# A graph attention stack on one core: neighbour lists split by the upper and lower 64 rows, and more row tiles worked on over all nodes

## The chip, the core and the metric

The kernel runs on one core of a Trainium2 chip. TensorE (PE, with its weight loads as PEld), VectorE (DVE), ScalarE (ACT), GpSimd (POOL) and SyncE (SP) each work through their own queue and wait for one another by semaphores; SP and POOL issue nearly all DMAs. The metric is the device time of one execution in microseconds.

## The reference

Four graph attention layers follow one another on 4096 nodes with 256 features. `adj` (4096 x 4096) is one on the diagonal and, by chance, in one place of 256. Layers 0 and 1 have four heads of width 64, layer 2 two heads of width 128, layer 3 one score with a positive and a negative softmax. Cut to one layer:

```
h = x @ W                                   # per head
e = leaky_relu(s1[:, None] + s2[None, :])   # slope 0.2; s1, s2: dots of h with two vectors
att = softmax(where(adj, e, -inf), axis=1)
x = layernorm(x + att @ h)                  # layer 3: x + elu([att @ x, -att_neg @ x] @ fc_W)
```

## The kernel before

**Tiles and lists.** The nodes make 32 row tiles of 128 rows (P = 128, NT = 32). For a row tile, only nodes that at least one of its rows has as a neighbour matter, some 39% of all. `lists` (L293-486) reads the adjacency as int32, turns it into uint8 masks (L385), marks for each source tile j and row tile which nodes are hit (L389, `places` L394-425), counts their places with small matmuls, and packs (`pack`, L427-462). Packing builds a one-hot per source tile (L440) and multiplies it with the mask and three digits of the node number (L446), up to three list tiles per PSUM bank; ScalarE copies them out (L453). The result is, for each row tile, 13 list tiles of 128 nodes (NG = 13) with their masks (`maskC`) and node numbers (`idx`). `windows` (L106-127) bounds which list tiles a source tile can land in: the first six list tiles (FRONT) hold only nodes of the first 17 tiles (MIX). A count that does not fit raises a flag, upon which dense layers would run.

**A row tile of a layer** takes 14 positions, its own 128 nodes at position 6 and the 13 list tiles, in two halves of 7. `RowTile.load` (L632) has SP fetch the edge row S, the mask and the own rows, and POOL one indirect DMA per list tile (L647), each of which gathers 128 rows of `vals` (values and scores) into a slot `G`. `place` (L615) spreads the positions over slots from two pools (g0: 16, g1: 14), two positions per slot in layers 0 to 2 and one in layer 3. `half` (L651) makes the weights: ScalarE one activation per position and head, 128x128 (L712; L690 in layer 3), VectorE the products of the head that is kept as an exponential (L704, L708) and the mask (L681, with the mask copied to PSUM at L666; L714; L692, L694). TensorE then multiplies. In layers 0 and 1 the values are the stationary operand (65 columns) and the weights move (128), so the sum comes out transposed (L724), and `copy` and `back` (L744-758) turn it with ScalarE and four transposes. In layers 2 and 3 the 128x128 weights are stationary and 129 or 257 value columns move (L727). Every fp32 matmul is two records in the trace.

**Whole blocks.** Some blocks of four row tiles are worked on over all 32 source tiles instead of lists (`WHOLE`, L99: three blocks in layer 2, one in layer 3). `whole_rows` (L982) is a generator; one unit is one source tile, with 128x512 weights (L1016-1024) and matmuls for four row tiles (L1027). It needs no gathers.

**Order of the work.** Each engine's queue follows the program. `run` (L489) projects all 32 tiles for layer 0 while the first 10 lists are built (LEAD), then runs layer 0 and builds one further list per tile; `part` (L812) loads tiles m and m + 1 and then does half a tile, with the projection for the next layer of tiles that are done. `half_with_whole` (L859) adds units by a pace (`whole`, L804). `close` (L919) ends a layer and begins the next: it loads first halves of the next layer's tiles, finishes the last tile, and in layer 2 runs 10 units of layer 3 ahead. `norm` (L1049) normalises tiles in groups (GROUPS) with VectorE.

Of the kernel before, what the change touches and what calls it, by code (L numbers as in the profile page):

```python
# [70 lines left out]
NG = 13  # L71
NP = NG + 1
CAP = NG * P
HALF = NP // 2

GROUPS = (((24, 4),), ((28, 2),), ((16, 2), (17, 1), (20, 2), (24, 1), (31, 2)), ((28, 1), (31, 4)))
LEAD = 10
MIX = 17
FRONT = 6
NODES = tuple(MIX * P if t < FRONT else N for t in range(NG))  # L80
MC = P + 4
# [6 lines left out]

LOGS = (3, 3, 2, 1)
# [3 lines left out]
KEXP = 10.0  # L93

# [4 lines left out]
WHOLE = ((), (), (3, 7, 6), (7,))  # L99
# [6 lines left out]
def windows():  # L106

    share = 1.0 - (1.0 - 1.0 / 256.0) ** P
    mean, sd = P * share, (P * share * (1.0 - share)) ** 0.5
    dev = 4.5  # L110
    out = {}
    for m in range(NT):
        for j in range(NT):
            if j == m:
                continue
            if j < MIX:
                n = sum(q != m for q in range(j))
                lo = mean * n - dev * sd * n ** 0.5
                hi = mean * (n + 1) + dev * sd * (n + 1) ** 0.5
            else:  # L120
                n = sum(q != m for q in range(j, NT))
                lo = CAP - mean * n - dev * sd * n ** 0.5
                hi = CAP - mean * (n - 1) + dev * sd * (n - 1) ** 0.5
            a = max(0, int(lo // P))
            b = min(NG - 1, int((hi - 1) // P))
            out[m, j] = (a, b - a + 1)
    return out
# [3 lines left out]
assert all(a >= FRONT for (m, j), (a, _) in WINDOW.items() if j >= MIX)  # L131
WMAX = max(n for _, n in WINDOW.values()) * P
# [7 lines left out]
def kernel(ctx: ExitStack, tc: tile.TileContext, ins: dict, out: bass.AP):  # L140
# [11 lines left out]
        "shift2": const.tile([P, 1], F32, name="shift2"),  # L152
        "shift3": const.tile([4, 4], F32, name="shift3"),
        "zero": const.tile([4, 4], F32, name="zero"),
        "maskC": dram.tile([NT, P, NP, MC], U8, name="maskC"),
# [8 lines left out]
    nc.vector.memset(shared["shift2"], -2.0 * KEXP)  # L164

# [28 lines left out]
class Program:  # L194


    def __init__(self, tc, ctx, ins, out, shared):
        self.tc, self.nc, self.ins, self.out, self.shared = tc, tc.nc, ins, out, shared
        self.ctx = ctx
        self.wpool = self.pool("w", 2)  # L200
        self.small = self.pool("small", 1)
        self.io = self.pool("pio", 2)
        self.g0 = self.pool("g0", 16)
        self.wp = self.pool("wp", 5)
        self.ld = self.pool("ld", 4)
        self.ep = self.pool("ep", 2)
        self.ptwo = [self.pool(f"ptwo{k}", 2, space=PSUM) for k in range(2)]
        two, one, last = (self.pool(f"pair{k}", 2 - (k > 0), space=PSUM) for k in range(3))
        self.pfour, self.pthree, self.pmask = Turns((two, one, two, last)), Turns((two, one, two)), last
        self.masks = None  # L210
        self.banks = self.pfour
# [81 lines left out]
    def lists(self, ctx):  # L293
# [21 lines left out]
        for k, sh in enumerate((8, 4, 0)):  # L315
# [21 lines left out]
        nc.gpsimd.affine_select(out=bt[:, :, :MIX], in_=bt[:, :, :MIX], pattern=[[NT, BT], [1, MIX]],  # L337
                                compare_op=ALU.is_gt, fill=0.0, base=0, channel_multiplier=-1)
        nc.vector.tensor_scalar(bt[:, :, MIX:], bt[:, :, MIX:], -1.0, None, op0=ALU.mult)

        nc.gpsimd.affine_select(out=bt[:, :, MIX:], in_=bt[:, :, MIX:], pattern=[[-NT, BT], [-1, NT - MIX]],
                                compare_op=ALU.is_ge, fill=0.0, base=-MIX, channel_multiplier=1)


        lo = cst.tile([P, NT, NT], F16, name="lo")
        wid = cst.tile([P, NT, NT], F16, name="wid")
        nc.gpsimd.memset(lo, 0.0)
        nc.gpsimd.memset(wid, 0.0)
        for j in range(NT):
            m = 0  # L350
            while m < NT:
                if m == j:
                    m += 1
                    continue
                e = m
                while e < NT and e != j and WINDOW[e, j] == WINDOW[m, j]:
                    e += 1
                a, n = WINDOW[m, j]
                nc.gpsimd.memset(lo[:, m:e, j], a * P - 1.0 - (CAP if j >= MIX else 0))
                nc.gpsimd.memset(wid[:, m:e, j], float(n * P))  # L360
                m = e
        limit = cst.tile([P, NP], F32, name="limit")
        nc.vector.memset(limit[:, :FRONT], float(MIX * P - 1))
        nc.vector.memset(limit[:, FRONT:], float(N - 1))
        total = cst.tile([P, NT], F32, name="total")
        bad = cst.tile([P, BT, NT], F32, name="bad")
        nc.vector.memset(bad, 0.0)

        class Block:
            def __init__(self, blk):  # L370
                self.blk = blk
                self.mk = mkp.tile([P, NT, BT, MC], U8, name="mk")
                self.red = wk.tile([P, BT, NT], F32, name="red")

            def prepare(self, part):
# [5 lines left out]
                for q in range(q0, q1, 2):  # L381
# [4 lines left out]
                nc.vector.tensor_copy(mkw[:, q0:q1, :, P // 4:],  # L386
                                      digw[:, q0:q1].rearrange("p (j t o) -> p j t o", t=1, o=1)
                                      .to_broadcast([P, JG, BT, 1]))
                nc.vector.tensor_reduce(self.red[:, :, q0:q1].rearrange("p t j -> p j t"),  # L389
                                        mkw[:, q0:q1, :, :P // 4], AX.X, ALU.max)  # L390
# [3 lines left out]
            def places(self):  # L394
                blk = self.blk
                if any(blk in w for w in WHOLE):
                    nc.sync.dma_start(out=shared["maskW"][blk], in_=self.mk)
                hit = wk.tile([P, BT, NT], BF16, name="hit")
                nc.vector.tensor_scalar(hit, self.red, 0.0, None, op0=ALU.is_gt)
                flat = hit.rearrange("p t j -> p (t j)")  # L400
                nc.vector.memset(flat[:, blk * BT:blk * BT + (BT - 1) * (NT + 1) + 1:NT + 1], 0.0)
                pt = prog.bank(prog.pthree)
                nc.tensor.matmul(pt[:, :P], flat, ones, start=True, stop=True)
                totals = wk.tile([P, P], BF16, name="totals")
                nc.scalar.copy(totals, pt[:, :P])
                pq = prog.bank(prog.pthree)
                nc.tensor.matmul(pq[:, :P], tri, flat, start=True, stop=False, skip_group_check=True)
                nc.tensor.matmul(pq[:, :P], totals, bt.rearrange("p t j -> p (t j)"), start=False, stop=False,
                                 skip_group_check=True)
                nc.tensor.matmul(pq[:, P:P + BT], totals, tot, start=False, stop=True, skip_group_check=True)  # L410
                ms = slice(blk * BT, (blk + 1) * BT)
                self.place = wk.tile([P, BT, NT], F32, name="place")
                here = self.place
                nc.vector.tensor_tensor(here, pq[:, :P].rearrange("p (t j) -> p t j", t=BT), lo[:, ms, :],
                                        op=ALU.subtract)
                nc.vector.tensor_tensor(here, here, hit, op=ALU.mult)
                nc.vector.tensor_copy(total[:, ms], pq[:, P:P + BT])

                for col in (wid[:, ms, :], None):
                    off = wk.tile([P, BT, NT], F32, name="off")  # L420
                    if col is None:
                        nc.vector.tensor_scalar(off, here, 0.0, None, op0=ALU.is_lt)
                    else:
                        nc.vector.tensor_tensor(off, here, col, op=ALU.is_gt)
                    nc.vector.tensor_tensor(bad, bad, off, op=ALU.max)

            def pack(self, it):  # L427
                m, mk = self.blk * BT + it, self.mk
                cm = cmp_.tile([P, NP, MC], U8, name="cm")
                order = [j for j in range(NT) if j != m]  # L430
                touches = {}
                for j in order:
                    a, n = WINDOW[m, j]
                    for k in range(a, a + n):
                        touches.setdefault(k // 3, []).append((j, k))
                accs = {}
                for j in order:
                    a, n = WINDOW[m, j]
                    oh = ohp.tile([P, WMAX], BF16, name="oh")
                    nc.vector.tensor_scalar(oh[:, :n * P], iota[:, :n * P], self.place[:, it, j:j + 1], None,  # L440
                                            op0=ALU.is_equal)
                    for k in range(a, a + n):
# [3 lines left out]
                        nc.tensor.matmul(accs[b][:, s * MC:(s + 1) * MC], oh[:, (k - a) * P:(k - a + 1) * P],  # L446
                                         mk[:, j, it, :].bitcast(FP8), start=touches[b][0] == (j, k),
                                         stop=touches[b][-1] == (j, k), skip_group_check=True)
                        if touches[b][-1] == (j, k):
                            e = min(3, NG - 3 * b)  # L450
                            got = accs[b][:, :e * MC].rearrange("p (s c) -> p s c", c=MC)
                            o = 3 * b + (3 * b >= FRONT)
                            last = nc.scalar.activation(cm[:, o:o + e, :], got, AF.Copy, scale=EDGE / 2.0)  # L453

                with tc.issue_after(last.ins):
                    nc.scalar.copy(cm[:, FRONT, :], mk[:, m, it, :])
                nc.sync.dma_start(out=shared["maskC"][m], in_=cm)

                t = wk.tile([P, NP], F32, name="t")
                nc.vector.scalar_tensor_tensor(t, cm[:, :, P], 16.0, cm[:, :, P + 1], op0=ALU.mult, op1=ALU.add)  # L460
                nc.vector.scalar_tensor_tensor(t, t, 16.0, cm[:, :, P + 2], op0=ALU.mult, op1=ALU.add)
                nc.vector.tensor_tensor(shared["idx"][:, m, :], t, limit, op=ALU.min)
# [1127 lines left out]
```

## Time and profile before

| | us |
|---|---|
| runs shown | 2251.94, 2260.22, 2251.93; median 2251.94 |
| profiled execution, span | 2249.3 |
| busy in it: PE, PEld, DVE, ACT, POOL | 2014.0, 1834.3, 1786.6, 1737.9, 1494.4 |
| gathers (L647, 1456) | from 101.3 to 2219.6; mean 1.017 each |
| gathers of layers 0, 1, 2, 3 (416, 416, 260, 364) | from 101.3, 783.6, 1313.0, 1681.2 |

The profile is one execution, seen by instruction: line, engine, operation, output and inputs, start and length. A group's mean is the length of one instruction; since instructions of an engine overlap at their ends, the distance between starts is what one costs a full queue, and it is a little shorter. The profiled execution's own time is not measured apart from its span; the span is 2.6 us under the median of the runs, which hold what lies before the first and after the last instruction. "issue" means that the engine waited for nothing that the profile shows.

### The profile page before, as it was taken

Reading aid. Unit: us, or ns where it says so; the run is one execution under the profiler, and the core shown is the slowest. Engines: PE = TensorE matmul, PEld = TensorE weight load, DVE = VectorE, ACT = ScalarE, POOL = GpSimd, SP = SyncE. Lnnn points to the kernel's source line nnn. Section 1 sums busy time; section 2 is a strip of 40 time slices with the busy share of each in tenths; the row PEclk is TensorE's granted clock in tenths of the full one; section 3 lists DMA queues with packets and bytes.
Section 4 is the critical chain, followed back from the end, with each engine's and each line's share of the span. In section 5 each row is a group of like instructions: output and inputs, shape, how many; then the busy total and the mean of one; then the engine's idle time right before and its main releaser. Section 6 shows DMA issues by size and latency. Waiting matters only on the chain. (4 is left out here: it accounts for less than half of the span.)

```text
span 2249.3 us, 49137 instructions
## 1 busy us (share of the span) xinstructions
PE 2014.0 (90%) x15689; PEld 1834.3 (82%) x15689; DVE 1786.6 (79%) x5060; ACT 1737.9 (77%) x4989; POOL 1494.4 (66%) x1597
## 2 busy tenths in 40 slices
PE   4878889989999969988899898989999999999995
PEld 2658788878899859988888798989998888788784
DVE  2889899999999959987988886887876566566566
ACT  4778988988789859987888776987876677667664
POOL 2107655656677777777777777777773477777773
PEclk7999999999999989999999999999999999999998
DMA  8879877777566665666665666777777688888884
GB/s 284 258 245 360 272 219 250 254 247 228 146 170 191 174 202 168 182 175 175 173 185 162 172 167 171 226 209 223 223 227 225 200 282 280 249 284 270 262 248 130
DMA packets 250319, 492.99 MB, mean 219 GB/s; under 512 B 44385, under 2 KB 156610, under 8 KB 249666
## 3 DMA queue, kind: packets, MB, share of 16 engines
q0 software_dynamic: 81536, 245.30, 38.3%
q1 hardware_dynamic: 163906, 240.26, 33.3%
q10 hardware_dynamic: 4608, 4.20, 0.5%
q8 instruction: 126, 2.06, 0.4%
q14 instruction: 143, 1.17, 0.2%
HBM read 437.05 MB, written 52.54 MB: 218 GB/s over the span
## 5 line engine op out<-in xcount | busy, mean ns | idle before, releaser
L647 POOL DMA_INDIRECT G<-vals,idx x1456 | 1480.7, 1017 | 715.7 <-issue 221.1
L712 ACT ACTIVATE w<-S,G 128x128 f32<-128x128 f32 x3248 | 1001.6, 390 | 140.6 <-DMA G<-vals,idx 101.6
L724 PE MATMUL bank<-w,G 128*65 128x128 f32 x7168 | 837.8, 276 | 59.7 <-DVE w L681 59.3
L724 PEld LDWEIGHTS bank<-w,G 128*65 128x65 f32 x7168 | 798.7, 140 | 69.9 <-DVE w L681 68.4
L681 DVE SCALAR_TENSOR_TENSOR w<-w,bank 128x1792 f32<-128x1792 f32 x256 | 514.6, 2013 | 13.4 <-ACT w L712 11.2
L727 PE MATMUL bank<-G,w 128*128 128x257 f32 (+1 forms) x2660 | 490.8, 342 | 25.7 <-ACT z L1102 13.6
L727 PEld LDWEIGHTS bank<-G,w 128*128 128x128 f32 x2660 | 431.9, 195 | 73.2 <-ACT z L1102 16.4
L1027 PE MATMUL bank<-vw,pw 128*128 128x129 f32 (+1 forms) x2048 | 298.5, 301 | 3.7 <-issue 2.3
L1027 PEld LDWEIGHTS bank<-vw,pw 128*128 128x128 f32 x2048 | 273.6, 191 | 20.1 <-issue 2.8
L690 ACT ACTIVATE w<-S,G 128x128 f32<-128x128 f32 x385 | 137.8, 393 | 136.8 <-DMA G<-vals,idx 90.0
L440 DVE TENSOR_SCALAR oh<-iota,place 128x256 bf16<-128x256 f16 (+2 forms) x992 | 221.8, 298 | 9.4 <-PE bank L446 9.1
L704 DVE TENSOR_TENSOR w<-S,G 128x256 f32<-128x256 f32 x384 | 151.9, 416 | 69.9 <-DMA G<-vals,idx 66.5
L446 PE MATMUL bank<-mk,oh 128*128 128x132 fp8e4 x2336 | 192.1, 226 | 13.8 <-ACT cm L453 7.0
L557 PE MATMUL bank<-wext,xT 128*128 128x268 f32 (+3 forms) x640 | 176.9, 409 | 16.9 <-ACT xT L548 14.1
L446 PEld LDWEIGHTS <-oh 128*128 128x128 bf16 x2336 | 146.9, 99 | 50.4 <-DVE oh L440 12.7
L385 ACT ACTIVATE mk<-raw 128x1024 uint8<-128x1024 int32 x128 | 130.5, 1051 | 28.0 <-DMA raw<-in_adjB_dram 27.7
L557 PEld LDWEIGHTS bank<-wext,xT 128*128 128x128 f32 x640 | 117.2, 200 | 36.0 <-ACT xT L548 16.9
L1017 DVE SCALAR_TENSOR_TENSOR pw<-pw,mw 128x512 f32<-128x512 f32 x192 | 127.6, 689 | 18.2 <-ACT pw L1016 17.5
L1016 ACT ACTIVATE pw<-Sw,d 128x512 f32<-128x512 f32 x192 | 133.2, 711 | 7.5 <-PE bank L1027 7.0
L714 DVE SCALAR_TENSOR_TENSOR w<-w,mk 128x896 f32<-128x896 f32 x80 | 86.6, 1086 | 41.1 <-ACT w L712 37.9
L1024 DVE TENSOR_TENSOR pw<-pw,mw 128x512 f32<-128x512 f32 x64 | 43.6, 691 | 85.4 <-ACT pw L1023 48.0
L692 DVE TENSOR_TENSOR w<-w,mk 128x896 f32<-128x896 f32 x55 | 60.0, 1091 | 59.5 <-ACT w L691 58.2
(140 smaller groups left out, 1563.3 us busy)
## 6 DMA issues: line engine op xcount, KB each, us to landing
raw<-in_adjB_dram SPq DMA_DIRECT2D x128, 512.0 KB
mk<-maskC SPq DMA_DIRECT2D x112, 231.0 KB
G<-vals,idx POOLq DMA_INDIRECT x1456
S<-edge SPq DMA_DIRECT2D x64, 256.0 KB
vw<-vals SPq DMA_DIRECT2D x96, 129.0 KB
xp<-y SPq DMA_DIRECT2D x96, 128.0 KB
y<-xp SPq DMA_DIRECT2D x96, 128.0 KB
mw<-maskW SPq DMA_DIRECT2D x20, 528.0 KB
```

Source lines behind the costliest of these rows:

```text
L440: nc.vector.tensor_scalar(oh[:, :n * P], iota[:, :n * P], self.place[:, it, j:j + 1], None, op0=ALU.is_equal)
L446: nc.tensor.matmul(accs[b][:, s * MC:(s + 1) * MC], oh[:, (k - a) * P:(k - a + 1) * P], mk[:, j, it, :].bitcast(FP8), start=touches[b][0] ...
L557: nc.tensor.matmul(pp[:, :c1 - c0], self.xT[:, k, :], wext[:, k, c0:c1], start=(k == 0), stop=(k == KT - 1 and brow is None))
L647: nc.gpsimd.indirect_dma_start(out=self.place(pos), out_offset=None, in_=sh["v"][n][:NODES[t], :], in_offset=bass.IndirectOffsetOnAxis(ap= ...
L681: nc.vector.scalar_tensor_tensor(pair, pair, LEAST, mh2, op0=ALU.max, op1=ALU.mult)
L690: nc.scalar.activation(w[0][:, k, :], S[:, 0, :], AF.Relu, bias=d(k, 0))
L704: nc.vector.tensor_tensor(w[h][:, k:k + 2, :], S[:, h:h + 1, :].to_broadcast([P, 2, P]), dd[:, :, V + T + h:V + T + h + 1].to_broadcast([P ...
L712: nc.scalar.activation(w[h][:, k, :], S[:, h, :], AF.Exp, bias=d(k, h))
L724: nc.tensor.matmul(accs[0][:Wd, h * P:(h + 1) * P], v, w[h][:, k, :], **how)
L727: nc.tensor.matmul(a, w[h][:, k, :], v, **how)
L1016: nc.scalar.activation(p, S[:, h], AF.Exp, bias=d)
L1027: nc.tensor.matmul(accs[it][:, c:c + Wd], p[:, it, :], v[:, c:c + Wd], start=(j == 0 and h == heads[0]), stop=(j == NT - 1), skip_group_ch ...
```

## The change

The rows of a tile are taken as an upper and a lower 64. A node is in one of three classes: hit by upper rows only, by lower rows only, or by both. Lists become five pairs and three mixed tiles. In a pair, one gathered tile of 128 nodes serves the upper 64 rows and another the lower 64, and both share one 128x128 tile of weights and mask (a unit); mixed tiles and the own tile serve all rows. So a row tile has 14 gathered or own tiles as before but 9 units instead of 14: 4 in the first half (own, three pairs), 5 in the second (two pairs, three mixed). Nodes over the five pairs spill into the mixed tiles.

Activations and matmuls of a pair come as two of 64 rows (columns) each. In layers 0 and 1 the weights are now the stationary operand and 65 value columns move, so the sum comes out straight and `copy` and `back` are gone. Masks and weights are as long as the units: 512 and 640 columns per head instead of 896. Lists read from 23 instead of 17 tiles in their first half. Slots hold a whole half tile (layer 3: four positions), 4 + 4 slots instead of 16 + 14. Block 7 (row tiles 28-31) of layer 1 is worked on whole by a new generator `whole_heads`, which takes the weight as a maximum of two products instead of an exponential; in layer 3 block 6 (24-27) joins block 7. With a whole block in layer 1, its end runs as layer 2's does: ten units of layer 2 ahead.

```
-NG = 13
-NP = NG + 1
-CAP = NG * P
-HALF = NP // 2
+HP = P // 2
+NPAIR = 5
+NMIX = 3
+NPACK = NPAIR + NMIX
...
+HALF = 7
+FIRST = 3
+UNITS = (1 + FIRST, NPACK - FIRST)
+FULL = ((0,), tuple(range(NPAIR - FIRST, NPACK - FIRST)))
+PAIRS = (tuple(range(1, 1 + FIRST)), tuple(range(NPAIR - FIRST)))
...
-MIX = 17
-FRONT = 6
-NODES = tuple(MIX * P if t < FRONT else N for t in range(NG))
-MC = P + 4
+MIX = 23
+MC = P + 8
...
+TWOS = ((3, 0), (2, 1))
...
+PER = tuple(HALF if n < 3 else 4 for n in range(4))
+SLOT = max(p * r for p, r in zip(PER, ROW))
...
-WHOLE = ((), (), (3, 7, 6), (7,))
+WHOLE = ((), (7,), (3, 7, 6), (7, 6))
...
+    hit = 1.0 - (1.0 - 1.0 / 256.0) ** HP
+    one, both = hit * (1.0 - hit), hit * hit
...
+        n = max(j - 1, 0), min(j + 1, NT - 1)
+        lo, hi = reach(one, *n)
...
+        c, d = reach(both, *n)
+        if hi > cap:
+            c, d = min(c, least + max(0.0, lo - cap)), max(d, most + spill + hi - cap)
...
+        out.append((a, b - a + 1, e, f - e + 1))
...
-        self.g0 = self.pool("g0", 16)
+        self.g0 = self.pool("g0", 4)
...
-                nc.vector.tensor_copy(mkw[:, q0:q1, :, P // 4:],
...
-                nc.vector.tensor_reduce(self.red[:, :, q0:q1].rearrange("p t j -> p j t"),
-                                        mkw[:, q0:q1, :, :P // 4], AX.X, ALU.max)
+                for u in range(2):
+                    nc.vector.tensor_reduce(self.red[:, u, :, q0:q1].rearrange("p t j -> p j t"),
+                                            mkw[:, q0:q1, :, u * HP // 4:(u + 1) * HP // 4], AX.X, ALU.max)
...
+                here = wk.tile([P, 2, BT, NT], F32, name="here")
+                nc.vector.tensor_tensor(here, at[:, :2], each(lo, 2, BT, NT), op=ALU.subtract)
+                nc.vector.tensor_tensor(here, here, cls[:, :2], op=ALU.mult)
+                nc.vector.tensor_tensor(here, here, move, op=ALU.add)
...
+                    nc.vector.tensor_scalar(oh[:, :len(ks) * P], iota[:, :len(ks) * P], self.place[:, it, j:j + 1],
+                                            None, op0=ALU.is_equal)
...
-        self.g1 = self.pool("g1", 14)
+        self.g1 = self.pool("g1", 4)
...
+    def slot(self, half, s):
...
+            pool = L.prog.g1 if n > 0 and half else L.prog.g0
+            self.slots[half, s] = pool.tile([P, SLOT], F32, name="G")
...
+        for k in range(1 - half, HALF):
+            pos = half * HALF + k - 1
             nc.gpsimd.indirect_dma_start(
-                out=self.place(pos), out_offset=None, in_=sh["v"][n][:NODES[t], :],
+                out=self.place(half, k), out_offset=None, in_=sh["v"][n][:N if half else MIX * P, :],
                 in_offset=bass.IndirectOffsetOnAxis(ap=sh["idx"][:, m, pos:pos + 1], axis=0))
...
+    def parts(self, half):
+
+        out, k = {}, 0
+        for u in range(UNITS[half]):
+            if u in PAIRS[half]:
+                out[u] = [(slice(0, HP), self.place(half, k)), (slice(HP, P), self.place(half, k + 1))]
+                k += 2
+            else:
+                out[u] = [(slice(0, P), self.place(half, k))]
+                k += 1
+        return out
...
+            for u in range(U):
+                for rows, g in parts[u]:
+                    nc.scalar.activation(w[0][:, u, rows], S[:, 0, rows], AF.Relu, bias=d(g, 0))
...
+            turns = ((3, 0), (1, 2)) if n < 2 else ((0,), (1,))
+
+
+        for t, heads in enumerate(turns):
+            for us in (FULL[half], PAIRS[half])[::-1 if t == 1 and (half == 1 or n < 3) else 1]:
+                for h in heads:
+                    for u in us:
+                        for rows, g in parts[u]:
+                            a = accs[h][rows, :Wd] if n == 3 else accs[0][rows, h * Wd:(h + 1) * Wd]
+                            nc.tensor.matmul(a, w[h][:, u, rows], g[:, h * Wd:(h + 1) * Wd],
+                                             start=half == 0 and u == 0 and (n == 3 or h == turns[0][0]),
+                                             stop=half == 1, skip_group_check=True)
...
-            for m in range(4 if following.n == 3 else 1):
+            for m in range(4 if following.n == 3 else 2 if WHOLE[self.n] else 1):
...
+    def whole_heads(self):
...
+            for up, flat in TWOS:
+                bu, bf = prog.bank(prog.pwhole), prog.bank(prog.pwhole)
...
+                for j in range(NT):
+                    fetch(j + 4)
+                    mj = mws[j - j % JG][:, j % JG, :, :P]
+                    v = vs.pop(j)
+                    p = {}
+                    for h in (up, flat):
+                        p[h] = prog.dp.tile([P, BT, P], F32, name="pw")
+                        nc.vector.scalar_tensor_tensor(p[h], S[:, h], c[:, j, h:h + 1], mj, op0=ALU.max, op1=ALU.mult)
+                    how = dict(stop=j == NT - 1, skip_group_check=True)
+                    for it in range(BT):
+                        nc.tensor.matmul(bu[:, it * Wd:(it + 1) * Wd], p[up][:, it, :],
+                                         v[:, up * Wd:(up + 1) * Wd], start=j == 0 and it == 0, **how)
+                        nc.tensor.matmul(bf[:Wd, it * P:(it + 1) * P], v[:, flat * Wd:(flat + 1) * Wd],
+                                         p[flat][:, it, :], start=j == 0 and it == 0, **how)
+                    yield
...
```

## The prediction

> **What bounds the kernel now.** I read the page's busy shares first (TensorE 90%, VectorE 79%, ScalarE 77%, POOL 66%: nothing decides), then the starts of the gathers on POOL, which cut the run into stages, then the table by stretches for these stages. Its columns: stretch, length, busy us (and instructions) of PE, PEld, DVE, ACT and POOL, granted clock, DMA share, GB/s.
>
> ```profile
> 0.00:163.00 163.00, 113.77 (x975) 85.75 (x975) 108.73 (x484) 105.95 (x252) 19.43 (x146) 0.87 0.81 262
> 163.00:645.00 482.00, 430.68 (x4300) 394.31 (x4299) 464.96 (x1383) 417.00 (x1240) 307.28 (x302) 0.98 0.75 243
> 645.00:783.50 138.50, 130.71 (x1141) 125.49 (x1139) 127.33 (x305) 125.23 (x436) 104.73 (x108) 1.00 0.65 179
> 783.50:1313.00 529.50, 466.52 (x3916) 436.63 (x3917) 444.46 (x1003) 435.81 (x1465) 402.46 (x417) 0.96 0.63 177
> 1313.00:1681.00 368.00, 348.66 (x2846) 336.01 (x2845) 291.92 (x766) 292.71 (x810) 287.58 (x260) 0.98 0.73 208
> 1681.00:2219.60 538.60, 511.23 (x2463) 445.61 (x2462) 332.29 (x1036) 354.67 (x771) 372.30 (x364) 0.98 0.82 253
> ```
>
> Rows 2 and 3 are layer 0, with and without list building; rows 4 to 6 are layers 1, 2 and 3 by the gathers. To 645 us VectorE is the full engine (465 of 482). After that the small POOL share misleads, as POOL's timeline shows (start, length, idle before):
>
> ```profile
> 1009.92 0.95 POOL L647 DMA_INDIRECT G<-vals,idx  x1 [0.30 <-issue]
> 1011.17 0.95 POOL L647 DMA_INDIRECT G<-vals,idx  x1 [0.31 <-issue]
> 1012.43 0.95 POOL L647 DMA_INDIRECT G<-vals,idx  x1 [0.30 <-DVE mv L1057]
> ```
>
> A gather every 1.2535 us, and 414 of layer 1's 415 gaps are this 0.30: POOL cannot go faster. 416 x 1.2535 = 521 of the 529 us. In layer 2 the 260 gathers are as dense (258 gaps of 0.30) but take 1.106 us: 360 of 368 us, TensorE being full as well. Layer 3 is TensorE, in the chain that ended last:
>
> ```profile
> 1801.81 6.07 PE bank L727 x28
> 1807.88 1.73 PE bank L1027 x8
> 1809.61 6.07 PE bank L727 x28
> 1815.68 1.73 PE bank L1027 x8
> ```
>
> 7.8 us per half tile, 15.6 per tile, while POOL asks 13 x 1.2535 = 16.3: both bind. The span is 2249.3 us; the median of the runs shown is 2251.9, so I add 2.6 to a worked-out span.
>
> **TensorE prices.** From the chain: 6.07 / 28 = 0.217 us per record of 257 moving columns, two records per fp32 matmul; 0.1115 for 129 columns, 0.109 for 128, 0.061 for the 65-column transposes of L757 (starts in the trace). A 128-column fp32 weight load sets the pace where little moves: L278, with two moving columns, starts every 0.112 us at 820 us. Half that for 64 columns is my estimate.
>
> **The open price: pairs.** A list tile still takes 14 matmuls per head, but ten now fill one half of the output rows each. No row shows two matmuls on separate halves. A narrow one alone is no cheaper (L589, four output columns: next start 0.109 us later, as between full ones). So a pair costs between one and two records' time. I take one: the two touch different array columns, weights and PSUM rows, and no row shows a resource that they share. This is the choice on which the forecast hangs; the other end is the first rival. A list tile of layer 3 then costs 2 heads x 2 records x (4 + 5) x 0.217 = 7.8 us instead of 12.1; of layer 2, 4.0 instead of 6.2.
> [...]
>
> **Part by part**, starts of VectorE instructions as prices: 1.93 us for 1792 elements, 1.00 for 896, 0.335 for 256, 0.20 for 128, one-hots 0.163, 0.196, 0.229 for 1, 2, 3 tiles (0.033 each more).
>
> *Lists.* By the two window formulas a row tile goes from 73 to 118 list matmuls and its one-hots from 206/32 = 6.4 to 7.9 us. Placing a block gains 13 operations of 256 and 9 of 128 elements and loses some: +5.9 us. Index arithmetic +0.25 per tile; the digit copies (0.4 x 4 per block) go. Before 163 us: ten lists and three blocks, 15 + 18 + 2.5 - 4.5 = 31 us on VectorE, 84% busy there after 50 us; between 14 (idle time takes it) and 37: **+28**. TensorE's 45 x 10 x 0.06 = 27 us lies beside.
> *Layer 0 with lists.* VectorE per tile: lists +2.9; masks of 1024 and 1280 elements, on the line through 896 and 1792, 2 x (1.135 + 1.40) instead of 4 x 1.93, -2.65; exponent products 0.20 + 0.47 + 0.335 + 0.47 = 1.47 instead of 6 x 0.335 + 2 x 0.20 = 2.4; mask copies -0.17: -0.85 for 22 tiles: **-19**. ScalarE loses 10 x 3 x 0.053 us and the 0.47 copy, TensorE the transposes; both lie under VectorE. From 645 on, POOL's 1.2535 stays: 0.
> *Layer 1.* 28 x 13 x 1.2535 = 456, plus the 8 us over the pure rate. The whole block adds 64 units with two L1017-like masks (0.69 us) on VectorE. These read two SBUF inputs, and in layer 2 gathers that overlap L1017 take 1.19 us against 1.01 for the others; there 219 us of such work cost POOL 41 us, so 88 us cost 16. TensorE's 64 units x 4 tiles x 0.39 (per tile and pair of heads: 0.112 + 0.056 + 0.109 + 0.112, the longer of each load and the matmul above it) = 100 us and VectorE's 88 lie under POOL, since 28 tiles at 10 us or less leave both below 390. Handover 3 us: 483 against 529.5: **-46**. Were POOL not the bound, nothing would be gained here. SP's extra v and mask loads queue ahead of the next tile's edge and mask rows; layer 2 has the same mix now and its gathers do not starve.
> *Layer 2.* POOL 326 + 36 (masks 2 x (0.60 + 0.74) instead of 4.0 us per tile): 362: **-6**. TensorE falls below it, 349 - 20 x 2.2 = 305. The ten units run ahead fill the handover.
> *Layer 3.* POOL 24 x 13 x 1.2535 + 28 (mask locks as now) + 8 = 427. TensorE 24 x 7.8 + 128 x 1.73 = 409, beneath. Two waits are added. Lists read from 23 instead of 17 tiles in a first half, so the first gathers need tile 22, one before the last of layer 2: normalising, projecting and storing it ends some 22 us after layer 2's last gather, by estimate (from that layer's last matmul at 1741.5 to the first gather that needs all rows at 1760.5 the same work takes 19 us now). All of layer 3's gathers stand behind it on POOL. And a first half takes two of four g0 slots, so the third tile's first half waits for the first tile's matmuls: 15 us by estimate (5 of landing, as in the chain, 5 for weights and masks, 5 on TensorE), with the first second halves queued behind. 22 + 427 + 15 = 464 against 538.6: **-75** (now 49 us of gaps lie there). Two more finishes at the end: **+3**.
>
> Sum: 2249.3 + 28 - 19 - 46 - 6 - 75 + 3 = 2134, as a time **2137 us**. Its own range, by the bounds above and 20 us for layer 3's balance: 2075 to 2190.
>
> **Rivals.**
> *Pairs run one after the other.* Then layer 3 binds on TensorE: -4 x 12.1 + 64 x 1.73 = +62 us, layers 2 and 3 need 860 + 62 - 12 (less left over from layer 1) = 910 busy, with 15 to 46 us idle (46 now): 925 to 956 against 906.6, and the 37 us saved before are mostly spent: 2236 to 2267, say 2252. For it: narrow matmuls save nothing alone. Against: different columns.
> *Pairs serial and their loads exposed (slower).* L560's two records start 0.325 us apart, where L557 with as many columns needs 0.221: a load stands bare when the array is split. If that holds for column halves, 800 records in layer 2 and 960 in layer 3 pay 0.053 (half of L560's 0.104; at most all of it) us more: +93, 2345 (from 2300, where only layer 3 pays, to 2440). It decides from 0.006 us per record, given the first rival. Against: L560 splits rows, not columns.
> *Slots too coarse.* A half is released as one or two slots, two tiles deep in layers 0 and 3: 20 gathers, 26 us, from landing to release. If halves take longer, 2.5 us per tile of layer 3 is lost: 2137 + 60 = 2197.
>
> **Numbers.** Forecast 0.62, serial pairs 0.17, exposed loads 0.13, slots 0.08. A measurement of this kernel tells about 0.5% from no change, that is 2241 to 2263. The serial rival splits 0.05 / 0.07 / 0.05. Faster 0.62 + 0.08 + 0.05 = 0.75, same 0.07, slower 0.18. Range 2070 to 2270: it holds the forecast but for a low tail, the slots and nearly all of the serial case.
>
> **What would show it.** Right: matmuls of 64 output columns whose starts come two per 0.217 us in layer 3; gathers at 1.25 us from about 790 to 1275; a POOL gap of some 20 us before layer 3; VectorE full to about 670. Wrong: starts 0.217 apart each, TensorE full through layer 3, POOL waiting there; or 0.27 and more apart. Wrong in another way: the first all-row gathers far after 190 us, or POOL gaps in every tile.

## The result and the profile after

The change made the kernel slightly slower: 2267.94 us median (2258.2 to 2278.29) against 2254.31 for before in the same rounds, ratio 1.0052 (95% interval 1.0035 to 1.007); beside the experiments it was run once more, 1.0034 (1.0013 to 1.0054). The forecast was 2137, ratio 0.95. Ten of the eighteen runs below (e1 to e4, e9 to e12, e16, e17: the second group) came from chips on which before, too, takes nearly a quarter longer (2761 to 2793 us), so their times are set only beside before and beside each other.

The stretches of after that answer to the table shown of before (same columns; cut 2 us behind the first all-row gather, about the end of the lists, at the first gather of layer 1, of layer 2, at its last, at the first and last of layer 3):

```profile
0.00:214.00 214.00, 148.63 (x1480) 121.76 (x1480) 147.19 (x585) 113.13 (x254) 16.82 (x80) 0.83 0.72 235
214.00:760.00 546.00, 452.57 (x5248) 414.46 (x5249) 465.57 (x1483) 349.95 (x1159) 291.24 (x300) 0.74 0.63 194
760.00:899.00 139.00, 116.56 (x1079) 99.98 (x1077) 94.73 (x287) 103.25 (x411) 106.09 (x109) 0.68 0.67 186
899.00:1374.00 475.00, 415.00 (x4384) 363.00 (x4383) 372.51 (x945) 330.64 (x1265) 363.75 (x366) 0.87 0.71 196
1374.00:1736.00 362.00, 336.90 (x2996) 309.39 (x2996) 277.37 (x788) 292.72 (x873) 275.46 (x260) 0.98 0.76 217
1736.00:1778.70 42.70, 41.02 (x272) 32.77 (x271) 36.35 (x184) 21.15 (x60) 0.16 (x2) 1.00 0.46 139
1778.70:2226.40 447.70, 428.89 (x2277) 315.94 (x2279) 260.32 (x812) 318.88 (x721) 317.15 (x312) 0.97 0.86 275
2226.40:2258.40 32.00, 10.82 (x70) 6.90 (x66) 19.61 (x94) 6.38 (x18) 1.05 (x1) 0.73 0.15 47
```

| stretch | before | forecast | after |
|---|---|---|---|
| to the first all-row gather | 163 | 191 | 214 |
| layer 0 with lists | 482 | 463 | 546 |
| layer 0, rest | 138.5 | 138.5 | 139 |
| layer 1 | 529.5 | 483 | 475 |
| layer 2, its gathers | 368 | 362 | 362 |
| gap ahead of layer 3 | (in 538.6) | 22 | 42.7 |
| layer 3, its gathers | 538.6 | 442 | 447.7 |
| tail | 30 | 33 | 32 |

Layers 1 to 3 came as forecast but for the gap. All that they win is lost before 760 us, and the column that changed there is the granted clock: 0.74 instead of 0.98. VectorE, full before, is busy for 466 of 546 us. Layer 1 still goes at POOL's pace, on POOL's timeline:

```profile
1099.19 0.95 POOL L714 DMA_INDIRECT G<-vals,idx  x1 [0.30 <-issue]
1100.44 1.06 POOL L714 DMA_INDIRECT G<-vals,idx  x1 [0.30 <-issue]
1101.81 0.94 POOL L714 DMA_INDIRECT G<-vals,idx  x1 [0.30 <-issue]
```

In layer 3, by the chain that ended last, the 28 records of a half take 3.96 or 4.68 us, where they took 6.07; 16 to 24 records of whole blocks stand between them:

```profile
1899.81 3.96 PE bank L819 x28
1903.78 3.67 PE bank L1102 x16
1907.44 4.68 PE bank L819 x28
1912.12 5.20 PE bank L1102 x24
```

So pairs do run at the same time: in the trace two records of 64 columns, one on each half, start 6 or 7 ns apart and the next two 0.210 us later (257 moving columns). The choice on which the forecast hung was right. The halves take 8.64 us per tile instead of 7.8, because a step from a 128-column record to a 64-column one costs more: 0.309 instead of 0.217 us with 257 moving columns, 0.205 instead of 0.112 with 65. So the step itself costs 0.093 us more. The way back costs 0.10 us (0.310 instead of 0.210 with 257 moving columns), and the records next to a change are 0.05 and 0.10 us apart beyond the usual. With five changes in the two halves of a tile, the 0.84 us come to some 0.17 us each.

What a half clock does in layer 0 shows within one tile. First three stretches of after, cut where the granted clock changes (same columns as above):

```profile
404.70:418.30 13.60, 13.60 (x108) 12.60 (x109) 9.64 (x30) 9.53 (x38) 4.62 (x5) 0.50 0.61 216
418.30:428.60 10.30, 8.01 (x130) 7.37 (x129) 9.29 (x28) 4.30 (x16) 7.77 (x9) 1.00 0.53 141
428.60:442.20 13.60, 13.58 (x106) 12.51 (x107) 11.49 (x50) 8.81 (x35) 4.72 (x5) 0.50 0.37 99
```

TensorE's timeline over them (start, length, line; last the idle time before and what ended it):

```profile
404.63 3.88 PE L819 MATMUL bank<-G,w 128*128 128x65 f32 x28 [2.31 <-DVE w L763]
408.75 3.89 PE L819 MATMUL bank<-G,w 128*64 128x65 f32 x28
...
413.09 2.55 PE L819 MATMUL bank<-G,w 128*128 128x65 f32 x28
415.57 2.11 PE L510 MATMUL bank<-mk,oh 128*128 128x136 fp8e4 x17
417.47 1.55 PE L630 MATMUL bank<-wext,xT 128*128 128x268 f32 x4
418.95 1.51 PE L819 MATMUL bank<-G,w 128*64 128x65 f32 x28
420.29 6.02 PE L510 MATMUL bank<-mk,oh 128*128 128x136 fp8e4 x99
428.62 3.89 PE L819 MATMUL bank<-G,w 128*128 128x65 f32 x28 [2.31 <-DVE w L763]
```

TensorE waits once in this row tile, 2.31 us for VectorE's mask (L763), and the clock is halved behind it; in the 546 us of the stretch it is halved 23 times. The two turns that follow (a turn is the 28 records of two heads in one half tile), of a second half, take 3.9 us each, though TensorE is hardly idle (busy for 13.60 of the 13.60 us). At full clock such a turn takes 2.17 us, in four cases of after and here in e13:

```profile
468.54 2.17 PE L819 MATMUL bank<-G,w 128*128 128x65 f32 x28 [0.79 <-DVE w L763]
```

The turns of a first half, with fewer full records, take 2.55 us at half clock (413.09) and 1.51 at full (418.95). The clock comes back at 418.3 us, behind list matmuls and a projection (L510, L630); the long run of list matmuls then goes at full clock, up to the next wait.

### The profile page after: what moved, and what is told of

Its sections match the earlier page's. It is cut to its first block, busy times and chain, and to the rows that moved or that the text cites. A ratio compares the mean times of both kernels' runs of the same rounds, so it can differ in the third digit from the quotient of the medians.

```text
span 2258.4 us, 52873 instructions
## 1 busy us (share of the span) xinstructions
PE 1950.4 (86%) x17799; PEld 1664.2 (74%) x17799; DVE 1673.7 (74%) x5170; ACT 1536.1 (68%) x4755; POOL 1371.7 (61%) x1426
## 5 line engine op out<-in xcount | busy, mean ns | idle before, releaser
L714 POOL DMA_INDIRECT G<-vals,idx x1352 | 1366.1, 1010 | 846.3 <-issue 410.9
L819 PE MATMUL bank<-G,w 128*64 128x65 f32 (+5 forms) x9156 | 893.2, 300 | 130.4 <-DVE w L763 120.2
L819 PEld LDWEIGHTS bank<-G,w 128*64 128x64 f32 (+1 forms) x9156 | 737.4, 182 | 290.3 <-DVE w L763 141.5
L805 ACT ACTIVATE w<-S,G 128x128 f32<-128x128 f32 (+1 forms) x3080 | 828.9, 351 | 134.6 <-DMA G<-vals,idx 117.6
L1102 PE MATMUL bank<-vw,pw 128*128 128x129 f32 (+1 forms) x2560 | 416.0, 320 | 16.5 <-issue 6.0
L763 DVE SCALAR_TENSOR_TENSOR w<-w,bank 128x1024 f32<-128x1024 f32 (+1 forms) x240 | 322.8, 1346 | 23.2 <-ACT w L805 20.5
L504 DVE TENSOR_SCALAR oh<-iota,place 128x640 bf16<-128x640 f16 (+3 forms) x992 | 283.6, 350 | 60.7 <-PE bank L510 60.0
L510 PE MATMUL bank<-mk,oh 128*128 128x136 fp8e4 x3782 | 262.2, 232 | 6.8 <-ACT cm L516 3.4
L510 PEld LDWEIGHTS <-oh 128*128 128x128 bf16 x3782 | 247.1, 103 | 14.0 <-DVE oh L504 4.9
L630 PE MATMUL bank<-wext,xT 128*128 128x268 f32 (+3 forms) x640 | 204.1, 458 | 28.0 <-ACT xT L621 17.2
L630 PEld LDWEIGHTS bank<-wext,xT 128*128 128x128 f32 x640 | 131.7, 223 | 58.5 <-ACT xT L621 23.1
L773 ACT ACTIVATE w<-S,G 128x64 f32<-128x64 f32 (+1 forms) x329 | 104.8, 352 | 86.0 <-DMA G<-vals,idx 47.4
```

Source lines behind the costliest of these rows:

```text
L504: nc.vector.tensor_scalar(oh[:, :len(ks) * P], iota[:, :len(ks) * P], self.place[:, it, j:j + 1], None, op0=ALU.is_equal)
L510: nc.tensor.matmul(accs[b][:, s * MC:(s + 1) * MC], oh[:, i * P:(i + 1) * P], mk[:, j, it, :].bitcast(FP8), start=touches[b][0] == (j, k), ...
L630: nc.tensor.matmul(pp[:, :c1 - c0], self.xT[:, k, :], wext[:, k, c0:c1], start=(k == 0), stop=(k == KT - 1 and brow is None))
L714: nc.gpsimd.indirect_dma_start(out=self.place(half, k), out_offset=None, in_=sh["v"][n][:N if half else MIX * P, :], in_offset=bass.Indire ...
L763: nc.vector.scalar_tensor_tensor(pair, pair, LEAST, mh2, op0=ALU.max, op1=ALU.mult)
L773: nc.scalar.activation(w[0][:, u, rows], S[:, 0, rows], AF.Relu, bias=d(g, 0))
```

## The experiments

Theory 1: the clock is what lengthened layer 0. Rival A: VectorE's added list work. Rival B: slots of half tiles.

**Matmuls that fill TensorE's wait (e1, e2, e6).** In `pack`, ahead of the last list matmul of a tile, into columns that nothing reads; six in e1 and e6, twelve in e2:

```
+    for _ in range(6 if j == order[-1] and k == ks[-1] else 0):
+        nc.tensor.matmul(accs[b][:, 3 * P:], ident, ident, start=False, stop=False)
```

> After, plus six fp32 matmuls of the identity into unused PSUM columns ahead of the last list matmul of each row tile (12 records of 0.109 us, 1.3 us of TensorE that computes nothing used). Theory 1 (TensorE's clock): in after the granted clock falls once per row tile, behind a wait of 2.3 us; with the wait filled it stays up. Clock of the stretch of layer 0 with lists 0.95 or more instead of 0.74, stretch 470 to 490 us instead of 546, time 2185 to 2215 us. Rival A (VectorE's added list work is the cost): clock may rise, stretch stays 535 to 555, time 2260 to 2280. Rival B (half-tile slots starve the compute): the gaps of 6 to 12 us per tile on POOL stay, 2260 to 2280.

> As the kernel with six, with twelve such matmuls (2.6 us of TensorE per tile). Theory 1: clock 0.95 or more; the stretch no more than 15 us longer than with six, since TensorE still lies under VectorE. Rivals A and B: 2270 to 2300 us, the added work being the only difference from after.

> The kernel with six fp32 identity matmuls per row tile again, beside after. Theory 1 (TensorE's clock): stretch of layer 0 with lists at a clock of 0.95 or more and 55 to 75 us shorter than after's; time 0.965 to 0.98 of after's. Rivals A (VectorE's list work) and B (half-tile slots): within 0.995 to 1.01 of after.

e1: ratio 1.0316 (1.0254 to 1.0379); e2: 1.0294 (1.0245 to 1.0342). Their ratios stand beside none of after, but e11, of the same group if on another chip, has after's layer 0: from the first all-row gather to the last one-hot it takes 757 us at clock 0.69, with six matmuls 720 at 0.78, with twelve 697 at 0.81. e6: 2254.65 us, 0.999 (0.9973 to 1.0007), beside after at 1.0034. From the first all-row gather to the last one-hot 518.8 us at clock 0.82, after 534.0 at 0.76. The direction of theory 1, about a quarter of the size.

**Another order of the halves in layer 0 (e3, e7).**

```
+    each = [(u, *part) for u in us for part in parts[u]]
+    for u, rows, g in sorted(each, key=lambda e: e[1].start) if n == 0 else each:
```

> After, with the halves' matmuls of layer 0 in another order: all full and upper ones of a turn first, then the lower ones, so that no two of different column halves stand side by side. Same instructions, but TensorE loses the overlap: at most 40 records of 0.112 us, 4.5 us of TensorE per tile. Theory 1: clock of the stretch up from 0.74 to 0.9 or more and the stretch down from 546 to 480 to 505 us, time 2205 to 2230: a slower TensorE makes the kernel faster. Rivals A and B: nothing or a loss, 2265 to 2300.

> Layer 0's halves in serial order again, beside after. Theory 1: clock of the stretch 0.9 or more, 40 to 65 us shorter than after's, time 0.97 to 0.985 of after's. Rivals A and B: 1.0 to 1.015 of after.

e3: 1.0388 (1.0339 to 1.0437). e7: 2264.5 us, 1.0054 (1.0032 to 1.0075), clock 0.77. This turned out to be no test: 64-column records of layer 0 start 0.0367 us apart at full clock instead of 0.0305, where a loss of the overlap would have doubled that. The order hardly slows TensorE (busy 440 of the stretch's 538.6 us, 437 of 534 in e5), so it couldn't fill its waits.

**Before with less work (e4, e8).** In `half` of before:

```
-    for k in range(HALF):
+    for k in (0, 6) if n == 0 and half == 1 else range(HALF):
```

> Before, with the matmuls of five of the fourteen units of each row tile of layer 0 left out (units 1 to 5 of the second half; their weights and masks are still made), so that TensorE has 4.4 us less per tile. Theory 1: the clock of the stretch with lists falls from 0.98 to 0.75 to 0.88 and the stretch grows from 482 to 500 us or more although work is gone: 2270 us or more. Rivals A and B: the stretch stays at 482 or falls, 2230 to 2256 us.

> Before without the matmuls of five units per row tile of layer 0 again (beside the 2760 us of before it took 1.008 of before's time). Theory 1: clock of the stretch down from 0.98 to 0.75 to 0.88, the stretch 482 to 500 us or more, ratio to before 1.005 to 1.02. Rivals A and B: ratio 0.985 to 1.0.

e4: 1.0081 (1.0053 to 1.0109). e8: 2277.56 us, 1.01 (1.0071 to 1.0129). The kernel leaves out the matmuls of five units, so TensorE's work is less, and it is slower. Its stretch from the first all-row gather to the last one-hot (477.8 us at 0.97 in before, VectorE 460.76):

```profile
165.30:658.70 493.40, 379.11 (x3414) 333.92 (x3412) 462.77 (x1369) 408.95 (x1217) 298.27 (x303) 0.84 0.74 236
```

TensorE is 48 us less busy, VectorE has the same work, and the stretch is 15.6 us longer, with no lists changed and no slots. A and B can't explain it. The loss is smaller than the change's own.

**After itself (e5), the control.**

> After itself, as the control for the three kernels beside it: the chip of the first four runs took 2760 us for before, with idle stretches on every engine that no instruction explains, so their times can't be set beside 2268. On a chip like the first: 2268 us, ratio to before 1.005, clock of the stretch of layer 0 with lists 0.74. On one like the second: ratio 1.01 to 1.05.

2260.52 us, 1.0034; clock 0.76 in the stretch.

**Matmuls that stream (e9, e10, e13).** Why six fp32 matmuls did so little, I read from windows of 3.41 us, the step in which the granted clock changes in the trace (of the 98 stretches at clock 1.0 or 0.5 in after all but the last are multiples of it long). For each in layers 0 and 1 of after I took TensorE's busy share and a count of what streams: moving columns of the records that start in it, as a share of 2.4 per ns at full clock and 1.2 at half (at full clock records of 136 columns start 0.059 us apart, the 16-bit ones of 240 columns of e13 0.1025: 104 columns more in 0.0435 us; at half clock records of 136 columns start 0.113 us apart). It is a count and not a time: full fp32 records that follow without a pause reach 0.49 (257 columns in 0.217 us).

| clock in the window, in the next | windows | busy, median | streaming count, median (10 to 90%) |
|---|---|---|---|
| full, full | 160 | 1.00 | 0.42 (0.32 to 0.95) |
| full, half | 37 | 0.40 | 0.22 (0.03 to 0.31) |
| half, half | 107 | 0.94 | 0.38 (0.19 to 0.51) |
| half, full | 37 | 1.00 | 0.67 (0.49 to 0.88) |

Busy time hardly tells the last two rows apart; the streaming count does so better, though 16 of the 107 windows counted 0.5 or more. A full product record of after moves 65 columns in 0.112 us, 0.24 by this count; before's moved 128 in 0.109, 0.49. A busy TensorE alone didn't bring the clock back: it stayed at half behind 107 windows, busy 0.94 at the median, and 50 of them were busy for over 0.98. So the kernel got 16-bit matmuls of 240 columns (six behind each turn and eight in `pack`, twice as many in e10; the turns' edit):

```
+    for _ in range(6 if n == 0 else 0):
+        nc.tensor.matmul(accs[0][:, 272:512], heat[:, :P], heat[:, :240], start=False, stop=False)
```

> After, with 16-bit matmuls of 240 moving columns into unused PSUM columns (about 0.1 us each at full clock): six behind each turn of layer 0's matmuls, eight ahead of the last list matmul of a row tile, 3.2 us of TensorE per tile that computes nothing used. Why other than the six fp32 ones, which raised the clock of the stretch with lists only from 0.76 to 0.82 and shortened it by 15 us: counted over windows of 3.4 us of layers 0 and 1 in after, the clock is halved after windows in which columns stream through TensorE for a median 0.22 of the time and stays half at a median 0.38, though TensorE counts as 0.9 busy there; it returns at a median 0.70. Matmuls of 65 moving columns behind a 128-column fp32 load stream for a quarter of their time. Theory 1 in this form: clock 0.93 or more, the stretch down from 534 to 475 to 500 us, time 2195 to 2235. Rivals A (VectorE's list work) and B (half-tile slots): stretch 515 us or more, time 2250 to 2275.

> The same with twice as many (twelve behind each turn, sixteen per list): 6.4 us of TensorE per tile. Theory 1: clock 0.97 or more, stretch within 12 us of the one with half as many, 2195 to 2245. Rivals A and B: 2255 to 2300.

> The kernel with the 16-bit matmuls (six of 240 moving columns per turn, eight per list) again: the chip before took 2793 us for before, as in the first four runs. Theory 1 (the gate follows the columns that stream): clock of the stretch with lists 0.93 or more instead of 0.76, the stretch 475 to 500 us instead of 534, ratio to before 0.975 to 0.99. Rivals A and B: stretch 515 us or more, ratio 0.995 or more.

e9: 1.0377 (1.0295 to 1.0459); e10: 1.0668 (1.0591 to 1.0745). Twice the dose raised the clock of the stretch only from 0.82 to 0.84 and made the stretch longer, 772 instead of 719 us: against its forecast. e13: 2225.48 us, **0.9872** (0.9845 to 0.99). Its layer 0, cut at the first all-row gather, the last one-hot and layer 1:

```profile
218.20:711.10 492.90, 444.61 (x5909) 394.52 (x5906) 456.52 (x1463) 343.27 (x1130) 295.50 (x298) 0.94 0.70 213
711.10:856.50 145.40, 120.87 (x1388) 104.05 (x1385) 103.57 (x318) 109.95 (x437) 108.41 (x113) 0.90 0.70 191
```

VectorE's longest waits in the first of these stretches (line waited for, us, times, longest):

```profile
DVE w L763 <- ACT w L805: 14.4, 7, 3.6
DVE oh L504 <- PE bank L510: 10.0, 19, 1.4
```

The same view of after, from 214 to 760 us, its longest wait:

```profile
DVE oh L504 <- PE bank L510: 58.5, 41, 2.4
```

Work that nobody needs, and the kernel is 35 us faster than after (e5). At half clock TensorE gets to the list matmuls late, VectorE finds none of its 8 one-hot buffers free and stands (58.5 us in after, 10.0 in e13): that is the link.

That the clock follows the streaming count rests on the table alone. e13's matmuls also fill more time than e6's (3.3, 32 of 0.1025, instead of 1.3 us per tile), and in the second group twelve fp32 ones (e2, 2.6 us, 697 us at 0.81) shortened the stretch no less than the 16-bit ones (e9, 719 us at 0.82). Whether it was the kind or the amount stays open.

**Layers 2 and 3 in the other order (e11)**, the edit of e3 with `n >= 2`.

> After, with the matmuls of layers 2 and 3 ordered so that all full and upper ones of a turn come before the lower ones: same instructions, no two of different column halves side by side. If pairs run at the same time only because they stand side by side, layers 2 and 3 lose up to 10 records per head, turn and tile: 2.2 us per tile in layer 2 and 4.3 in layer 3; with TensorE as the bound there, layers 2 and 3 go from 884 us (1374 to the end) to 930 to 975, time 2310 to 2360. If the records of one half already overlap each other (in layer 0 the serial order changed TensorE's busy time by nothing), within 10 us of after.

1.0469 (1.0392 to 1.0547). In layer 3 64-column records with 257 moving columns start some 0.14 us apart at full clock, 0.104 in e5: a third more, not twice. Layers 2 and 3 take 1062 us, in e9 beside it 1044. At 0.14 us, where 128-column records take 0.217, records of one half overlap somehow too; how, I leave open. So the serial rival was priced too high even in its own case.

**Whole blocks as in before (e12, e15)**, in e15 with GROUPS of layers 1 and 3 to match.

```
-WHOLE = ((), (7,), (3, 7, 6), (7, 6))
+WHOLE = ((), (), (3, 7, 6), (7,))
```

> After with the whole blocks of before (none in layer 1, tiles 28 to 31 alone in layer 3), the pairs kept. The prediction's steps: layer 1 is POOL's, 32 x 13 x 1.2535 + 8 = 530 us (474 in after); layer 3 is POOL's too, 28 x 13 x 1.2535 + 28 + 8 = 492 (447.7), with TensorE less full: time 2268 + 55 + 44 = 2365. Rival, that the halves or TensorE bound layers 1 and 3: fewer whole units relieve TensorE of 62 us in layer 3 and of 100 in layer 1, time 2240 to 2300.

> After with the whole blocks of before (none in layer 1, tiles 28 to 31 alone in layer 3) and the normalisations grouped to match, the pairs kept (the earlier kernel of this kind lacked that grouping, and some of its rows were never normalised). The prediction's steps: layers 1 and 3 are POOL's, so layer 1 takes 32 x 13 x 1.2535 + 8 = 530 us (474 in after) and the gathers of layer 3 about 28 x 13 x 1.2535 + 28 + 8 = 492 (448): time 2260 + 55 + 44 = 2360. Rival, that TensorE or the half-tile slots bound layers 1 and 3: fewer whole units free 62 us of TensorE in layer 3 and 100 in layer 1, time 2240 to 2300.

e12 (1.0444) leaves some row tiles without their normalisation and isn't used. e15: 2323.73 us, 1.0296 (1.0279 to 1.0313), 63 us more than after in e5. Its layer 1 and the gathers of its layer 3:

```profile
888.30:1415.00 526.70, 419.99 (x3877) 353.70 (x3876) 336.93 (x879) 372.63 (x1447) 399.91 (x417) 0.68 0.63 171
...
1822.00:2302.00 480.00, 386.68 (x2005) 249.78 (x2005) 251.95 (x846) 279.97 (x670) 367.55 (x364) 0.91 0.84 262
```

Layer 1 is 52 us longer with TensorE at 0.68 clock and no fuller, layer 3's gathers 32. (Its layer 0, which the edit leaves nearly as it is, took 9 us less.) POOL sets both, as forecast for this number of tiles; pairs alone gain nothing in layer 1.

**Another last tile in layer 2 (e14)**, on top of e13:

```
-WHOLE = ((), (7,), (3, 7, 6), (7, 6))
+WHOLE = ((), (7,), (5, 3, 6), (3, 6))
```

> The kernel of the run before (streaming matmuls in layer 0, 2225 us) with other blocks taken over all nodes: blocks 5, 3, 6 instead of 3, 7, 6 in layer 2 and 3, 6 instead of 7, 6 in layer 3, and the grouping of the normalisations to match. So the last four list tiles of layer 2 are 28 to 31, which layer 3's first halves (nodes below tile 23) don't need, where it was 20 to 23. If the gap on POOL ahead of layer 3 (42 us in after, 22 forecast) is the wait for tile 22 of the layer before, it falls to 15 us or less and the time to 2190 to 2205 us. If something else holds it (slots, projections in general), 2215 to 2235.

2217.98 us, 0.9851 (0.982 to 0.9883). POOL's timeline at the start of layer 3:

```profile
1703.14 0.95 POOL L714 DMA_INDIRECT G<-vals,idx  x1 [16.59 <-ACT row L648]
...
1746.02 0.94 POOL L714 DMA_INDIRECT G<-vals,idx  x1 [21.71 <-DMA vals<-row]
```

The gap falls from 42.5 us in after (44.1 in e13) to 16.6, so it was the wait for tile 22. But 12 gathers on, the first one over all rows waits 21.7 us for the last rows of layer 2: one wait took the other's place. Some 7 us are left of 27, and the intervals of e13 and e14 overlap.

**More one-hot buffers (e16)**: `pool("oh", 16)` instead of 8.

> After with 16 buffers for the one-hots instead of 8 and nothing else. In after VectorE waits 53 us of the stretch of layer 0 with lists for list matmuls to free one of the 8 buffers (39 waits, at most 2.5 us each), 10 us with the streaming matmuls, 4 in before. If the half clock costs time only because VectorE stands still at these buffers, eight more (8 one-hots of 0.23 us, 1.8 us) take most of these waits away though the clock stays at 0.75: stretch 534 down to 495 to 510, ratio to before 0.985 to 0.995. If the late matmuls cost at other places as well (masks, evictions, slots), the stretch stays above 520 and the ratio above 0.998.

1.0344 (1.0295 to 1.0393). Beside e11, whose layer 0 is after's, VectorE's wait for a buffer falls from 121 to 41 us, its wait for the lists' eviction rises from 9 to 114, and the stretch is 733 instead of 757 us. Buffers move the wait; they don't replace the clock.

**All that paid (e17, e18)**: e14, 16 buffers, and ScalarE's activations of the first tile put behind those of the last projection (`issue_after`). The reason, on ScalarE's timeline of after:

```profile
157.45 1.46 ACT L805 ACTIVATE w<-S,G 128x64 f32<-128x64 f32 x5 [8.40 <-DMA G<-vals,idx]
159.48 0.35 ACT L805 ACTIVATE w<-S,G 128x64 f32<-128x64 f32 x1 [0.57 <-DMA G<-vals,idx]
159.73 0.49 ACT L516 ACTIVATE cm<-bank 128x408 uint8<-128x408 f32 x1
```

> All that paid or should: the streaming matmuls in layer 0, blocks 5, 3, 6 and 3, 6 over all nodes, 16 one-hot buffers, and the activations of layer 0's first half tile put behind those of the last projection (in after ScalarE waits 8.4 us at 149 us for that tile's gathers, with list evictions and projections queued behind, and every engine runs dry). If that wait is part of the 50 us by which the phase ahead of the all-row gathers grew, the first of these falls from 213 to 218 us to 203 to 210. Time 2195 to 2212 us, ratio 0.975 to 0.981; 2215 to 2225 if neither the buffers nor the order bring anything.

> The same kernel again, since the chip before took 2792 us for before. There the first all-row gather came at 204 us (209 to 220 us in the kernels without the new order of ScalarE's work), and the 16 buffers alone only moved VectorE's wait from the one-hot buffers (121 to 41 us) to the eviction of the lists (9 to 114 us). So on a chip like the first: phase 204 us, stretch with lists 485 to 495 us, time 2200 to 2212 us, ratio 0.975 to 0.981, if the 12 us of the phase come through; 2215 to 2225 if they are lost behind.

e17: 1.036 (1.0316 to 1.0404). e18: 2212.35 us, **0.9816** (0.9793 to 0.9838), the fastest here, at the upper end of its forecast (2200 to 2212 us, 0.975 to 0.981); its interval overlaps e14's. Its first all-row gather comes at 202.1 us (218.2 in e13), and the stretch with lists stays at 488.7.

## Why the prediction was wrong

The sum of the steps was 124 us under the span of after. By step:

- **Layer 0 with lists: -19 forecast, +57 measured** (first all-row gather to last one-hot: 477.8, then 534.9). The failed step is "ScalarE loses ..., TensorE the transposes; both lie under VectorE". TensorE's work was counted in instructions at full-clock prices, and as hidden it was set to nothing. It was cover only at full clock. With work and moving columns taken from it the clock fell from 0.97 to 0.74, and then VectorE stood behind it. With e13's added matmuls, at 0.94, 41 us come back (32 by e15, whose nearly unchanged layer 0 took 525 us where e5's took 534), and e8 shows a loss of the same kind, 15.6 us, without the change. Another 12 are VectorE's: masks (170.4 to 110.1 us in the stretch) and exponent products came as priced, but one-hots grew from 145.2 to 191.4, 0.279 us each where the line of 0.033 per tile gave 0.255. VectorE's work so fell by 5 (as busy time, 460.8 to 456.0) to 7 us instead of 19. The rest, some 20 us more of VectorE idle than in before, even at clock 0.94, isn't settled; rival B may be in it.
- **Phase ahead of it: +28 forecast, +48 measured** (163.4, then 211.7). VectorE's work in it, 145 against 109 us, grew by more than the 31 priced. On top, lists that read from 23 tiles let the first gather start at 149.7 instead of 101.3 us, and ScalarE stands 8.4 us behind it with evictions and projections queued. e18 takes away up to 16 us; how much of it the buffers gave isn't apart (e16, buffers alone, begins at 209.0, after at 213.2 in e5).
- **Layer 0 behind the last one-hot: 0 forecast, +10 measured** (142.4, then 152.8), all of it ahead of 760 us. From there POOL's pace holds, 139 us after 138.5, though the clock is 0.68: here, where POOL binds, the slow TensorE cost nothing.
- **Layer 1: -46 forecast, -54.5 measured; layer 2: -6 and -6.** Right, and for the reason given (e15).
- **Layer 3: 442 forecast for its gathers, 448 measured.** Pairs at one record's time, right; but that the sum came so close is partly luck. The steps between 128 and 64 columns, for which the sum has no term, add 0.84 us per tile, so TensorE is busy for 429 us and not 409, and is not beneath POOL, whose 312 gathers ask 411 at their mean length (1.0165 us and 0.30 between them; 28 us were priced for slower gathers, 20 came). The single wait of 15 us for slots did not come: up to 1988 us no gap is over 2.1. In its place and that of the 8 us priced beside it, POOL idles for 37 us in small gaps beyond its 0.30, and most of its waits for another engine are those for TensorE (from 1779 to 2226 us):

```profile
POOL G L714 <- PE bank L819: 28.6, 24, 5.9
```

- **The wait ahead of layer 3, 22, was mis-sized: 42.7**, with the mechanism right (e14).
- **Tail: +3 and +2.**

None of the three rivals came; the third, slots too coarse, is nearest to POOL's small gaps in layer 3. "First all-row gathers far after 190 us" stood in the list of signs, and it came; the clock stood in the tables read, and no step asked what the change would do to it.

## What to carry to other kernels

An engine that lies under another is hidden at its present speed: where a change makes TensorE's work shorter or moves fewer columns per weight load, look at the granted clock (0.97 to 0.74 in layer 0 here, 0.97 to 0.84 in e8, in the stretch with lists) and at the waits between its bursts before its cost is set to nothing. The sign in a trace is one line's records at two paces within a tile (28 in 2.2 and in 3.9 us); the test is a dose of useless matmuls, or leaving work out. Where the first work of a stage waits for the last rows of the stage before, count the next thing that waits for the same rows.

## What the hardware showed that was not expected

- A kernel with 5 of 14 units of layer 0's matmuls left out ran 1% slower (e8), and one with 3.3 us of useless 16-bit matmuls per row tile of layer 0 1.6% faster than after (e13, 0.9872 against 1.0034).
- In layers 0 and 1 of after the clock fell behind windows of 3.41 us that counted 0.22 streaming at the median and came back behind windows of 0.67; windows with a median busy share of 0.94 and 0.38 streaming left it at half.
- Two fp32 records on separate 64-column halves start 6 to 7 ns apart; changing between 128 and 64 columns costs 0.093 us at the step and some 0.17 us with the records next to it.
